# Separate buffers for the packed granules, the packed down weights and their repacked form, and a shift of when they are loaded, in a fused layernorm, S4 and int4 FFN kernel

## The chip, the cores and the metric

The kernel runs on one core of one Trainium2 chip. The metric is the device time of one execution in microseconds (us). A single profiled execution has its own time, which is given beside the median of the runs. Engines are called PE (TensorE), DVE (VectorE), ACT (ScalarE), POOL (GpSimd) and SP (SyncE, which here issues nearly all transfers, in one order, as a queue).

## The reference

One layer on an input of 2048 tokens by 1024 channels: a layernorm, and then the sum of the input, a state-space convolution (S4) and a gated feed-forward network (FFN) whose weights are 4-bit integers with a scale and a zero point for each group of 64.

```python
def dequantize(W_q, scale, zero):            # W_q: two 4-bit values per element
    hi = W_q >> 4 & 15
    lo = W_q & 15
    w = jnp.stack([hi, lo], axis=-1).reshape(out, half * 2).astype(scale.dtype)
    w = w.reshape(out, -1, GROUP)            # GROUP = 64
    return ((w - zero[:, :, None]) * scale[:, :, None]).reshape(out, half * 2)
...
g = jnp.einsum('bsh,ih->bsi', xn, dequantize(gate_Wq, ...))    # 2752 x 1024
u = jnp.einsum('bsh,ih->bsi', xn, dequantize(up_Wq, ...))
ffn = jnp.einsum('bsi,hi->bsh', silu(g) * u, dequantize(down_Wq, ...))
...
s4 = irfft(rfft(xn, 2 * L) * rfft(K, 2 * L))[..., :L] + D * xn  # K from the S4 parameters
return x + s4 + ffn
```

## The kernel before, in words

The weights come as 65 granules of 128x512 int32 (256 KB each; one int32 holds two 4-bit values). Granules 0 to 41 are the gate and up weights, two for each of the blocks 0 to 20; granule 42 is a mixed remainder; 43 to 62 are down weights in ten pairs; 63 and 64 are the last down weights (`G_WP` is 63). Gate/up and last granules also have a small tile of scales and zero points, sz.

A gate/up granule goes through these steps. `load_raw` (line 304) issues two transfers on SP, the packed granule into a tile raw and its sz. `unpack` (312) lets DVE split the 4-bit values into a tile w, two instructions. `scale_a` (346), called by `w_scale` in three parts of 4, 6 and 6 groups, lets ACT apply scale and zero point, 16 instructions. DVE then forms sums of quarters of w (`w_sums`), because the matrix product is done with seven products in place of eight. ACT writes the high half of each value in fp16 and DVE the rest (`w_hi`, `w_lo`, into tiles nat). `w_t` transposes the two nat tiles by DMA into a weight tile wf, which PE reads. There is a ring of four wf tiles; below, wf24 is the tile of granule 24.

The down granules are handled by `load_wd` (478), one unit u for each pair. `load` (485) brings the packed granule into a raw tile. `fetch_wd` (489) issues four transfers of scales into w, lets DVE split the packed values into int16 in a tile qn (two instructions), and transposes qn by DMA back into the raw tile. `dequant` (506) is two DVE instructions from that raw tile. Sums, `hi` (ACT) and `lo` (DVE, followed by a transfer to memory, WD) follow for seven parts. The two granules of the next unit are loaded and fetched in the course of the unit.

`gate_up` (623) is the main work on PE: for a block j and one half cp of the tokens it does seven products of 12 matmuls each (128x512), into the accumulation banks A, B, C and D; ACT copies banks between products (`A.copy(bD, bB)` gives "D<-B" in the trace) and DVE and ACT form the gated result in tiles ha, hb and s, which SP writes to memory (HF). One block takes about 36 us.

The loop at lines 1148 to 1169 runs over blocks 4 to 20 and both halves. Between the products of a half it advances the granules under way (`step_granules`), the down units (`wd_steps`) and the steps of the S4 kernel (`s4_steps`, tiles s4n, s4p). Here the instruction orders of DVE, ACT, PE and SP are pinned: every instruction of an engine is issued after the one that stands before it in the program (class `Engine`, 67 to 86). An instruction that waits therefore holds up all that stand behind it on that engine. All pinned instructions carry the line 82 in the profile, unpinned ones the line 77, and so tiles are told apart by name.

`granule` (1107) is the chain for one gate/up granule; each `yield` is one step. `queue` holds the granules still to do and `ahead` those that are loaded one ahead. Granule 63 is loaded in the loop just before its chain starts.

Buffers: `wtemp` (140) takes a tile from the pool in `home[kind]`. At line 1088 the kinds "raw" and "sz" get a pool raw2 on the left side of memory. Its ring of tag raw has four slots, which packed gate/up granules, packed down granules and qn tiles share in the order in which they are asked for; sz has two. A new tile in a slot waits for the last use of the old one.

```python
            szbufs[0] = 2
            home["raw"] = home["sz"] = more("left", "raw2", 4)
```

Of the kernel before, what the change touches and what calls it, by code (L numbers as in the profile page):

```python
# [26 lines left out]
I32 = mybir.dt.int32  # L27
I16 = mybir.dt.int16
# [5 lines left out]
P = 128  # L34
# [4 lines left out]
NJ = 21  # L39
# [3 lines left out]
G_WP = G_WD + 2 * NPAIR  # L43
# [5 lines left out]
SPG = 8  # L49
FETCH = {8: 15, 9: 15}  # L50
BEHIND = {4: 15}

XS = 64.0
WS = 1024.0
# [33 lines left out]
def build(nc, tc, x, xp, raw_d, sz_d, par_d, vct_d, tab_d, csrow_d, out):  # L88
# [3 lines left out]
    with es:  # L92
# [37 lines left out]
        right = lambda name, **k: ea.enter_context(tc.tile_pool(name=name, side="right", **k))  # L130
# [3 lines left out]

        we = ExitStack()
        weights = lambda side, name, **k: we.enter_context(tc.tile_pool(name=name, side=side, **k))
        home, szbufs = {"nat": weights("right", "nat", bufs=4)}, [4]
        home["raw"] = home["sz"] = home["w"] = weights("right", "dq", bufs=2)

        def wtemp(kind, shape, dtype, name):  # L140
            return home[kind].tile(shape, dtype, tag=kind, name=name, **({"bufs": szbufs[0]} if kind == "sz" else {}))

        early = ExitStack()
        hfp = early.enter_context(tc.tile_pool(name="hf", bufs=2))
# [155 lines left out]
        with ea:  # L300
# [1 line left out]
            rawt = {}  # L302

            def load_raw(gi):
                raw = wtemp("raw", [P, 16, 32], I32, f"raw{gi}")
                ld = SP
                ld.dma_start(raw, raw_d[gi].rearrange("p (a b) -> p a b", a=16))
                sz = wtemp("sz", [P, 2, 16], F32, f"sz{gi}")
                ld.dma_start(sz, sz_d[gi])
                return raw, sz  # L310
# [167 lines left out]
            def load_wd(u):  # L478


                pr, kq = divmod(u, 2)
                ga, gb = (G_WD + 2 * p + kq for p in (pr, pr + NPAIR // 2))
                tt, sub = V.tensor_tensor, ALU.subtract

                def load(gi):
                    raw = rawd[gi] = wtemp("raw", [P, 16, 32], I32, f"raw{gi}")
                    SP.dma_start(raw, raw_d[gi].rearrange("p (a b) -> p a b", a=16))

                def fetch_wd(gi):


                    raw = rawd.pop(gi)
                    w = wtemp("wd", [P, 8, 256], F32, f"w{gi}")
                    for i in range(2):
                        for b in range(2):
                            SP.dma_start(w[64 * b : 64 * b + 64, 4 * i : 4 * i + 4].rearrange("p f c -> p (f c)"),
                                        SZT[gi - G_WD, 1 - i, b].rearrange("c h -> (c h)").partition_broadcast(64))
                    q = wtemp("raw", [P, 16, 2, 32], I16, f"qn{gi}")
                    low = raw.bitcast(I16).rearrange("p a (b c) -> p a b c", c=2)[:, :, :, 0]
                    V.tensor_scalar(q[:, :, 0, :], low, 4, 15, ALU.logical_shift_right, ALU.bitwise_and)  # L500
                    V.tensor_scalar(q[:, :, 1, :], low, 15, None, ALU.bitwise_and)
                    qt = raw.bitcast(I16).rearrange("p a b -> p (a b)").rearrange("p (a b) -> p a b", a=8)
                    SP.dma_start_transpose(qt, q.rearrange("p a b c -> p (a b c)"))
                    return w, qt

                def dequant(w, qt):
                    x4 = w[:, 0:4]
                    tt(x4, qt.rearrange("p (f a) b -> p f (a b)", f=4), x4, sub)
                    tt(x4, x4, w[:, 4:8], ALU.mult)

                blocks = lambda w: w.rearrange("p f (m c) -> p f m c", m=2)
                nats = {}

                def hi(i, src):
                    nats[i] = wtemp("nat", [P, 7, 2, P], F16, f"nd{u}_{i}")
                    A.copy(nats[i][:, :, 0], src)

                def lo(i, src):
                    nat = nats.pop(i)
                    tt(nat[:, :, 1], src, nat[:, :, 0], sub)  # L520
                    SP.dma_start(
                        WD2[i - 1][:, :, pr, kq].rearrange("f p a c -> p f (a c)"), nat.rearrange("p f a c -> p f (a c)")
                    )

                nxt = [G_WD + 2 * ((u + 1) // 2 + o) + (u + 1) % 2 for o in (0, NPAIR // 2)] if u + 1 < NPAIR else None
                if u == 0:
                    load(ga)
                    load(gb)
                    yield
                    ready_wd[ga] = fetch_wd(ga)  # L530
                    yield
                    ready_wd[gb] = fetch_wd(gb)
                    yield
                ma = ready_wd.pop(ga)
                dequant(*ma)
                if nxt:
                    load(nxt[0])
                wa = blocks(ma[0][:, 0:7])
                yield
                sums(ma[0], True)  # L540
                hi(1, wa[:, :, 0])
                yield
                lo(1, wa[:, :, 0])
                tt(wa[:, :, 0], wa[:, :, 1], wa[:, :, 0], sub)
                hi(5, wa[:, :, 0])
                yield
                lo(5, wa[:, :, 0])
                yield
                mb = ready_wd.pop(gb)
                dequant(*mb)  # L550
                if nxt:
                    load(nxt[1])
                wb = blocks(mb[0][:, 0:7])
                yield
                sums(mb[0], True)
                hi(3, wb[:, :, 1])
                yield
                tt(wa[:, :, 1], wb[:, :, 1], wa[:, :, 1], sub)
                lo(3, wb[:, :, 1])
                hi(7, wa[:, :, 1])  # L560
                yield
                tt(wb[:, :, 1], wb[:, :, 1], wa[:, :, 0], sub)
                lo(7, wa[:, :, 1])
                hi(6, wb[:, :, 1])
                yield

                lo(6, wb[:, :, 1])
                hi(2, wb[:, :, 0])
                if nxt:
                    ready_wd[nxt[0]] = fetch_wd(nxt[0])  # L570
                yield
                lo(2, wb[:, :, 0])
                tt(wb[:, :, 0], wb[:, :, 0], wb[:, :, 1], sub)
                hi(4, wb[:, :, 0])
                yield
                lo(4, wb[:, :, 0])
                if nxt:
                    ready_wd[nxt[1]] = fetch_wd(nxt[1])
                yield
# [504 lines left out]
            we.close()  # L1084
            more = lambda side, name, bufs: weights(side, name, bufs=bufs, reuse_waits="tile")
            home["nat"], home["w"], home["wd"] = more("right", "nat2", 5), more("right", "w2", 1), more("right", "wd", 2)
            szbufs[0] = 2
            home["raw"] = home["sz"] = more("left", "raw2", 4)

            wd_steps = (None for u in range(NPAIR) for _ in load_wd(u))  # L1090
            s4_steps = s4()
# [15 lines left out]
            def granule(gi):  # L1107

                last_i = gi >= G_WP
                if not gi % 2:  # L1110
                    yield
                w_unpack(gi)
                w_scale(gi, 0)
                yield
                if gi + 1 in ahead:
                    rawt[gi + 1] = load_raw(gi + 1)
                w_scale(gi, 1)
                yield
                w_scale(gi, 2)
                yield  # L1120
                if not last_i:
                    w_sums(gi)
                yield
                wp_hi(gi - G_WP) if last_i else w_hi(gi)
                yield
                wp_lo(gi - G_WP) if last_i else w_lo(gi)
                if not last_i and gi % 2:
                    w_t(gi)
                yield
                yield  # L1130
                yield
                if not last_i and not gi % 2:
                    w_t(gi)
                yield
# [19 lines left out]
            for j in range(4, NJ):  # L1154
                for cp in range(2):
                    PE.pin = (j, cp) != (4, 0)
                    for n, _ in enumerate(gate_up(j, cp, wt[j])):
                        if n == 4 and queue:
                            if queue[0] == G_WP:
                                rawt[G_WP] = load_raw(G_WP)  # L1160
                            under_way.append(granule(queue.pop(0)))
                        if n == 2:
                            step_granules()
                        if n in (2, 4, 6) or n == 0 and waits is None:
                            next(wd_steps, 0)
                        if waits == "read" or n == 5 or n == 0 and cp and waits != "bank":
                            waits = s4_next()
                        if n != 2:
                            step_granules()
# [446 lines left out]
```

## Time and profile before

| what | value |
|---|---|
| median of 3 runs | 1281.69 us (1280.97 to 1282.39) |
| the profiled execution | 1286.51 us, its span 1284.7 us |
| mean granted clock of PE in it | 0.993 |
| PE busy | 1259.7 us, 98% of the span |
| DVE, ACT, POOL busy | 1020.2 us (79%), 676.5 us (53%), 184.3 us (14%) |
| HBM read and written | 132.88 MB and 94.84 MB |
| loads of packed granules (raw) | 65 of 256 KB, 4.0 us from issue to landing in the median |

A group of instructions in the profile is written engine, operation, out<-in, with the shapes as partitions x elements. An idle time stands in brackets behind an instruction, with the arrow to what ended it: "[0.47 <-ACT D L82]" says that the engine sat idle for 0.47 us until ACT's instruction on bank D. SPq is SP's queue, and its durations are those of issuing, not of the transfer.

### The profile page before, as it was taken

How to read it: one execution, taken by the hardware profiler on the slowest of the kernel's cores; microseconds unless marked ns; L12 is line 12 of the kernel's file. 1: busy time of each engine (PE TensorE's matmuls, PEld its weight loads, DVE VectorE, ACT ScalarE, POOL GpSimd, SP SyncE). 2: the span in 40 equal slices, each digit the busy share in tenths (PEclk: the TensorE clock that was granted, in tenths of full speed). 3: DMA queues.
4: the chain of work that ended last, by engine and by line, in shares of the span. 5: the costliest groups of instructions: out<-in, count | busy, mean ns of one | idle time of the engine just before them, and what ended most of it. 6: DMA issues, size and time to landing. Idle time of an engine off the chain costs nothing. (4 is left out here: it accounts for less than half of the span.)

```text
span 1284.7 us, 21385 instructions
## 1 busy us (share of the span) xinstructions
PE 1259.7 (98%) x8098; PEld 760.0 (59%) x8098; DVE 1020.2 (79%) x1391; ACT 676.5 (53%) x1219; POOL 184.3 (14%) x280
## 2 busy tenths in 40 slices
PE   7999899999999999999998999999999999999998
PEld 6644344444444444444443444467678888888887
DVE  7789975788888788779787886657669889779792
ACT  6777665665757656676576575620205433343330
POOL 2330010000010000101010001100000130366440
PEclk8999999999999999999998999999999999999999
DMA  6792829788895969799998998866868777999981
GB/s 233 195 209 50 184 92 207 191 227 207 207 252 133 266 148 247 192 224 248 238 243 198 260 246 185 251 231 200 307 201 317 254 236 217 257 288 257 289 175 50
DMA packets 358842, 276.59 MB, mean 215 GB/s; under 512 B 211851, under 2 KB 304851, under 8 KB 354643
## 3 DMA queue, kind: packets, MB, share of 16 engines
q1 hardware_dynamic: 336147, 263.17, 74.4%
q0 software_dynamic: 22016, 11.02, 7.1%
q8 instruction: 63, 1.03, 0.3%
q10 hardware_dynamic: 576, 1.05, 0.2%
q14 instruction: 40, 0.33, 0.1%
HBM read 132.88 MB, written 94.84 MB: 177 GB/s over the span
## 5 line engine op out<-in xcount | busy, mean ns | idle before, releaser
L82 PEld LDWEIGHTS <-wf 128*128 128x128 f16 x3000 | 287.3, 99 | 348.9 <-issue 11.5
L77 PEld LDWEIGHTS <-g 128*128 128x128 f16 x2940 | 287.6, 98 | 34.0 <-DVE g L77 0.6
L82 ACT ACTIVATE w<-w,sz 128x64 f32<-128x64 int32 x564 | 197.8, 428 | 66.8 <-DVE w L82 50.1
L82 PE MATMUL D<-x,wf 128*128 128x512 f16 x816 | 191.3, 385 | 2.2 <-ACT D L82 2.2
L77 PE MATMUL A<-b,g 128*128 128x256 f16 x1680 | 186.0, 273 | 0.3 <-DVE g L77 0.3
L82 PE MATMUL A<-x,wf 128*128 128x512 f16 x792 | 177.9, 380 | 5.0 <-DMA wf<-nat 4.6
L82 PE MATMUL C<-x,wf 128*128 128x512 f16 x804 | 179.1, 379 | 0.0
L77 ACT CAST g<-a 128x2560 f16<-128x2560 f32 x42 | 97.4, 2325 | 135.8 <-PE A L77 50.4
L82 DVE TENSOR_TENSOR w<-w 128x256 f32<-128x256 f32 (+1 forms) x244 | 132.7, 545 | 39.4 <-ACT w L82 32.3
L77 PEld LDWEIGHTS <-wf 128*128 128x128 f16 x960 | 86.0, 98 | 95.6 <-DMA wf<-nat 5.7
L77 DVE TENSOR_TENSOR g<-a,g 128x2560 f16<-128x2560 f32 x42 | 118.2, 2820 | 27.5 <-ACT g L77 27.5
L1468 POOL DMA_DIRECT2D out<-o x64 | 77.9, 2019 | 308.1 <-DVE o L77 288.3
L334 POOL TENSOR_SCALAR sz<-sz 128x16 f32<-128x16 f32 x43 | 19.4, 450 | 627.8 <-DMA sz<-in_sz 551.7
L82 ACT CAST nd<-w 128x896 f16<-128x896 f32 x70 | 65.3, 933 | 83.5 <-DVE w L82 70.0
L77 PE MATMUL D<-b,g 128*128 128x256 f16 x840 | 94.1, 273 | 0.0
L82 PE MATMUL B<-x,wf 128*128 128x512 f16 x396 | 90.9, 379 | 0.1
L82 DVE TENSOR_TENSOR nd<-w,nd 128x896 f16<-128x896 f32 x70 | 76.0, 1086 | 9.1 <-ACT nd L82 9.1
L82 ACT CAST nat<-w 128x896 f16<-128x896 f32 x62 | 55.3, 936 | 33.4 <-ACT B L82 17.0
L77 PEld LDWEIGHTS <-x 128*128 128x128 f16 x672 | 54.3, 98 | 20.9 <-issue 2.4
L82 DVE TENSOR_TENSOR nat<-w,nat 128x896 f16<-128x896 f32 x62 | 64.8, 1084 | 1.1 <-ACT nat L82 1.1
L77 DVE SCALAR_TENSOR_TENSOR p<-cv,p 128x512 f32<-128x512 f32 x32 | 22.0, 689 | 34.9 <-PE cv L77 23.4
L77 PE MATMUL cv<-band,x 128*128 128x256 f16 (+3 forms) x384 | 47.0, 272 | 2.0 <-DVE p L77 2.0
(181 smaller groups left out, 1451.1 us busy)
## 6 DMA issues: line engine op xcount, KB each, us to landing
a<-HF SPq DMA_DIRECT2D x28, 1280.0 KB, 7.4
WD<-nd SPq DMA_DIRECT2D x70, 448.0 KB, 4.0
b<-WD SPq DMA_DIRECT2D x49, 640.0 KB, 6.1
w<-SZT SPq DMA_DIRECT2D x80, 256.0 KB, 5.3
raw<-in_raw SPq DMA_DIRECT2D x65, 256.0 KB, 4.0
HF<-ha SPq DMA_DIRECT2D x54, 256.0 KB, 3.2
HF<-s SPq DMA_DIRECT2D x40, 256.0 KB, 3.2
HF<-hb SPq DMA_DIRECT2D x36, 256.0 KB, 3.2
```

Of the source, the lines that this page charges most:

```text
L77: return method(*args, **kw)
L82: self.last = method(*args, **kw)
L334: G.tensor_scalar(sz[:, 0], sz[:, 0], WS, None, ALU.mult)
L1468: G.dma_start(dst, o[:, q], accum_op=ALU.add)
```

## The change

A ring of four slots for all three kinds is replaced by kinds with buffers of their own: one for packed gate/up granules ("raw"), two for packed down granules ("rawd"), one for qn. The footprint is the same. Granules 8, 9 and 10 are loaded from this pool before the first down unit needs it; the dictionary `RAW` puts them into the buffers of the other two kinds.

With one buffer for a packed gate/up granule, the load of the next one moves in `granule` from before the second part of `w_scale` to before the third, one step later. Granules 63 and 64 are now among those that are loaded one ahead: granule 63 is loaded in the chain of granule 41, which is the one before it in the queue, and the separate load in the loop is gone. In `load_wd` the loads of the next unit's granules move from behind `dequant` to behind the first `lo` of the same granule, two steps later.

```diff
+RAW = {8: "qn", 9: "rawd", 10: "rawd"}
...
-        home, szbufs = {"nat": weights("right", "nat", bufs=4)}, [4]
+        home, own = {"nat": weights("right", "nat", bufs=4)}, {"sz": 4}
...
-            return home[kind].tile(shape, dtype, tag=kind, name=name, **({"bufs": szbufs[0]} if kind == "sz" else {}))
+            return home[kind].tile(shape, dtype, tag=kind, name=name, **({"bufs": own[kind]} if kind in own else {}))
...
             def load_raw(gi):
-                raw = wtemp("raw", [P, 16, 32], I32, f"raw{gi}")
+                raw = wtemp(RAW.get(gi, "raw"), [P, 16, 32], I32, f"raw{gi}")
...
                 def load(gi):
-                    raw = rawd[gi] = wtemp("raw", [P, 16, 32], I32, f"raw{gi}")
+                    raw = rawd[gi] = wtemp("rawd", [P, 16, 32], I32, f"raw{gi}")
...
-                    q = wtemp("raw", [P, 16, 2, 32], I16, f"qn{gi}")
+                    q = wtemp("qn", [P, 16, 2, 32], I16, f"qn{gi}")
...
                 dequant(*ma)
-                if nxt:
-                    load(nxt[0])
                 wa = blocks(ma[0][:, 0:7])
                 yield
                 sums(ma[0], True)
                 hi(1, wa[:, :, 0])
                 yield
                 lo(1, wa[:, :, 0])
+                if nxt:
+                    load(nxt[0])
...
                 dequant(*mb)
-                if nxt:
-                    load(nxt[1])
...
                 lo(3, wb[:, :, 1])
+                if nxt:
+                    load(nxt[1])
...
-            szbufs[0] = 2
-            home["raw"] = home["sz"] = more("left", "raw2", 4)
+            own.update(sz=2, raw=1, rawd=2, qn=1)
+            home["raw"] = home["sz"] = home["rawd"] = home["qn"] = more("left", "raw2", 1)
...
-                if gi + 1 in ahead:
-                    rawt[gi + 1] = load_raw(gi + 1)
                 w_scale(gi, 1)
                 yield
+                n = G_WP if gi == 2 * NJ - 1 else gi + 1
+                if n in ahead:
+                    rawt[n] = load_raw(n)
                 w_scale(gi, 2)
...
                         if n == 4 and queue:
-                            if queue[0] == G_WP:
-                                rawt[G_WP] = load_raw(G_WP)
                             under_way.append(granule(queue.pop(0)))
```

## The prediction

> **What bounds the kernel now.** I read the page first. TensorE (PE) is busy for 1259.7 of 1284.7 us, so at most 25 us can be had by removing waits anywhere, and every loss must appear as a new PE wait.
>
> ```profile
> span 1284.7 us, 21385 instructions
> PE 1259.7 (98%) x8098; PEld 760.0 (59%) x8098; DVE 1020.2 (79%) x1391; ACT 676.5 (53%) x1219; POOL 184.3 (14%) x280
> ```
>
> The change touches only the loop over blocks 4 to 20, which lies between 200 and 865 us. The table of windows gives PE 657.69 us busy there, so 665.00 - 657.69 = 7.3 us idle in that stretch. PE's list of waits for 160 to 870 us says on what:
>
> ```profile
> PE A L82 <- DMA wf<-nat: 4.6, 3, 2.9
> PE D L82 <- ACT D L82: 2.2, 1, 2.2
> PE cv L77 <- DVE p L77: 0.9, 1, 0.9
> PE A L82 <- DVE ha L82: 0.4, 1, 0.4
> ```
>
> The columns are total us, times, longest. The first line is weight tiles whose transposes land late (0.47 at block 12, 2.89 and 1.25 at block 17). The second is one wait at 800 us, the only one that the changed loads cause directly. The timeline from 788 to 802 us shows it:
>
> ```profile
> 792.60 1.68 SPq L82 DMA_DIRECT2D raw<-in_raw  x1
> ...
> 796.81 0.76 DVE L82 TENSOR_SCALAR w<-raw 128x512 int32<-128x512 int32 x2 [5.08 <-DMA raw<-in_raw]
> ...
> 798.30 1.43 ACT L82 ACTIVATE w<-w,sz 128x64 f32<-128x64 int32 x4 [9.99 <-POOL sz L336]
> ...
> 799.64 0.57 ACT L82 COPY D<-B 128x512 f32<-128x512 f32 x1
> 800.26 2.30 PE L82 MATMUL D<-x,wf 128*128 128x512 f16 x6 [2.22 <-ACT D L82]
> ```
>
> Granule 63 is loaded just before it is unpacked. VectorE (DVE) waits 5.08 us, ScalarE (ACT) stands behind it, ACT's copy into bank D comes late, and PE loses 2.22 us.
>
> The instruction orders of PE, DVE and ACT are the same in both builds; only SyncE's (SP's) queue is reordered and some waits differ. So the sum consists of (1) that load, (2) new waits for buffers, (3) weight transposes that meet other transfers ahead of them on SP.
>
> **The change part by part.**
>
> *1. Granule 63 loaded at granule 41, about one half-block earlier.* The 5.08 us on DVE and the 2.22 us on PE go. What is late next there: the block 20 weights, whose tile wf41 has 3.0 us between landing and need, and which now gets two loads ahead of it (0.42 + 0.40 us of issue by the 799 us pair): still 2 us in hand. I take **-2.2**, range -2.2 to -1.9.
>
> *2. One buffer for the repacked form (qn).* Of 40 instructions that write qn in 20 granules, four already waited for the previous granule's transpose; the tile's view says
>
> ```profile
>   DMA raw<-qn: 11.5, 4
> ...
> DMA to landing us min/median/max: 5.5/5.9/7.3
> ```
>
> In the four-slot ring the second qn of a pair mostly came to the slot of the first, so it waited already; I compared the waits of both builds, and only qn56 (block 11) is newly made to wait, for qn46's transpose. DVE's and then SP's timeline:
>
> ```profile
> 418.85 0.76 DVE L82 TENSOR_SCALAR qn<-raw 128x512 int16<-128x512 int16 x2
> ...
> 420.33 0.69 DVE L82 SCALAR_TENSOR_TENSOR hb<-hb,D 128x512 f32<-128x512 f32 x1 [0.47 <-ACT D L82]
> ...
> 435.81 0.76 DVE L82 TENSOR_SCALAR w<-raw 128x512 int32<-128x512 int32 x2 [2.90 <-DMA raw<-in_raw]
> ```
>
> ```profile
> 418.99 1.26 SPq L82 DMA_TRANSPOSE raw<-qn  x1
> ...
> 430.60 0.43 SPq L82 DMA_DIRECT2D raw<-in_raw  x1
> ...
> 431.86 1.27 SPq L82 DMA_DIRECT2D HF<-hb  x2
> ```
>
> qn46's transpose is issued at 418.99; two loads that now come ahead of it (raw22, sz22) add about 0.9; it lands 5.5 to 7.3 later, median 5.9, so at 425.8. DVE stood ready at 418.85: a stall of 6 to 7 us (bounds 419.9 + 5.5 - 418.85 = 6.6 and 8.4; without the 0.9, 5.6). DVE's order is fixed, so all behind it waits: the hb sum, the scaled weights, the second dequantisation. On its way the delay eats the idle time that DVE had: 0.47, 0.32 and 0.90 us up to 425, then 2.90 us at 435.81 for raw23. That last one is no free cover: raw23 itself is reissued behind the two HF transfers of 1.27 us and behind the late work, so it lands at 437.7 to 438.4, which agrees with 435.81 + 6.95 - 4.6 = 438.2. From there DVE and ACT run 2.0 to 2.6 us late. The next idle places on DVE (1.11 us at 442.31, 2.62 at 465.75) wait for ACT, which is delayed by the same chain, so they cover little. PE's margins down the road, each the need minus the end of its producer: 2.1 us at 441.4, 2.2 at 451.8, 1.7 for wf23 (458.2), 0.05 at 467.58, none at 477.08. PE's timeline there:
>
> ```profile
> 477.08 2.75 PE L82 MATMUL A<-x,wf 128*128 128x512 f16 x12 [0.38 <-DVE ha L82]
> ...
> 497.77 0.82 PE L82 MATMUL A<-x,wf 128*128 128x512 f16 x3 [0.47 <-DMA wf<-nat]
> ```
>
> So nearly the whole 2.0 to 2.6 reaches PE at 467 or 477: **+2.3**. Bounds: 3.5, if the landing takes 7.3 us and nothing is absorbed; and 0.5 from below, since a like wait, 4.08 us at 614.19, cost PE nothing, although there the next margins were wider (0.44 us at 627 and then none below 2). I stay near the upper part because 467.58 has no margin.
>
> A rule that speaks against this part: the Trainium skill, "Trainium Kernel Development and Optimization", Best Practices, advises two buffers so that transfers run beside computing. The row above, 11.5 us of DVE waiting in four places, agrees that a shared buffer makes DVE wait, but the 4.08 us of it at 614 cost PE nothing; by the rule every such wait is a loss and this part would cost all 6 to 7 us, by the row nothing.
>
> *3. wf25 (block 12).* SP's queue between the transposes of wf24 and wf25 (483.31 and 490.62) now holds raw26 and sz26, 0.9 us. PE already waits 0.47 there, so there is no margin. But if item 2 has delayed PE by 2.3, the need moves too, and only what the producers lose beyond that counts. I take **+0.7**; range -0.4 (the wait vanishes in PE's lateness) to +1.2.
>
> *4. wf35 (block 17).* raw51 leaves from ahead of these transposes:
>
> ```profile
> 676.19 0.39 SPq L82 DMA_DIRECT2D raw<-in_raw  x1
> ...
> 678.08 4.88 SPq L82 DMA_TRANSPOSE wf<-nat  x2
> ```
>
> Its 0.39 us and the gap of 0.09 behind it come off the 2.89 us wait: **-0.5**. Range -1.4 (also a 256 KB transfer less beside the transposes) to 0 (the weights themselves are late).
>
> *5. wf37 (block 18).* raw38 and sz38 (0.42 and 0.41 us at 700.70 and 701.22) now go between the two pairs of transposes at 702.80 and 714.78. The margin is 1.04 us and PE is 0.5 earlier by item 4: 0.83 + 0.5 - 1.04 = 0.3, with gaps between issues **+0.4**; range 0 to 0.9.
>
> *6. Other loads moved later.* Every gate/up granule is loaded one step later and every down granule about two. A load lands in 4.0 to 4.4 us; nearly all had 5 to 50 us in hand. The least is raw33, now behind a qn transpose: **0**, range 0 to +0.5. Odd weight tiles 13, 15, 19 and 39 lose a load ahead of them, but had margin: 0.
>
> Sum: -2.2 + 2.3 + 0.7 - 0.5 + 0.4 = **+0.7 us**. The profiled execution took 1286.51 us, 4.8 above the median of the runs, 1281.69; I put the change on both: 1287.2 profiled and **1282.4** as the median.
>
> **The rivals.** 0.2%, 2.56 us, is about what a measurement of this kernel can tell from no change; so 1279.1 to 1284.3 is "the same".
>
> *A, slower: the qn wait hits PE in full.* One place, block 11: if raw23's unpack starts more than 4.4 us late (after 440.2 instead of 438), PE's 0.05 us of margin at 467.58 passes everything on. With 4.4 in place of 2.3 the sum is +2.8, from which point it is slower; a landing of 7.3 us (+1.4) together with raw23 behind another HF issue of 1.27 makes item 2 5.0 and the sum +3.4: 1285.1. For it: no margin at two points. Against it: the median landing, 5.9.
>
> *B, faster: the qn wait is soaked up* as at 614.19. Then item 2 is 0 and PE keeps -2.2 - 0.5 + 0.4 + 0 to 0.7, so -2.3 to -1.6, or -2.7 if wf37 is in time: about 1279. If the 2.89 + 1.25 us at block 17 vanish too, because less is in flight, 1275.6. Against it: DVE's idle places behind 435 wait for ACT, which the same chain feeds.
>
> *C, the buffers do not matter.* PE is fed through a pipeline some 30 us deep; losses of 0.3 to 0.7 us on SP and the gain at 800 us cancel, or neither shows: 1281 to 1282. Same sign as my forecast, with no qn stall reaching PE.
>
> **How the numbers follow.** My forecast with its bounds (1279.5 to 1284.5) and C together 0.52; A 0.30; B 0.18, of which 0.05 below 1278. Range: with every item at its upper bound, and item 2 at 3.5, the sum is -1.9 + 3.5 + 1.2 + 0 + 0.9 + 0.5 = 4.2, 1285.9; B's 1279 without the 1.25 us at block 17 is 1277.7, and the rest of B lies below. So 1277.7 to 1286.0, which also holds A's 1285.1. Since A lies wholly above 1284.3 and B nearly wholly at or below 1279.1: faster 0.17, same 0.52, slower 0.31.
>
> **What the changed profile would show.** 1: no DVE wait for raw at 797, no PE wait for D at 800. 2: a DVE wait of 6 to 7 us for the transpose of qn near 419, the wait of 2.90 near 436 gone or smaller, new PE waits of 2 us at 467 or 477. 3: PE's wait for wf near block 12 about 1 us. 4: the 2.89 at block 17 near 2.4. 5: a PE wait below 1 us near 725. The qn tile's line should total about 18 us in 5 places. The forecast is wrong if the stall at 419 is absent, if it exceeds 8.4, or if transposes slow or speed up because other transfers now run beside them: SP's transposes take 4.3 to 6.3 us a pair, so each 1 us on wf25, wf35 or wf37 moves PE by about as much.

## The result, and the profile after

The changed kernel takes 1285.07 us (median of 17 runs, 1283.39 to 1286.72) against 1281.5 (17 runs of before, 1279.9 to 1284.73). The ratio is 1.0026, with a 95% interval of 1.0019 to 1.0032: slower by 3.3 us (3.6 between the medians). The profiled execution took 1286.03 us, 1.0 above its median.

The page of the changed kernel begins:

```profile
span 1284.3 us, 21381 instructions
PE 1258.2 (98%) x8098; PEld 759.2 (59%) x8098; DVE 1019.9 (79%) x1391; ACT 676.0 (53%) x1219; POOL 200.2 (16%) x280
```

The span is 0.4 us *shorter* than that of before, although the timed runs are 3.3 us longer. The profiled execution of before was an unlucky one, 5.0 us above its median, so the two spans cannot be set against each other. What can be compared is where each engine waits, and the time between the same two matmuls, since PE issues the same 8098 in both. PE's list of waits of the changed kernel, 160 to 870 us (total us, times, longest):

```profile
PE A L83 <- DMA wf<-nat: 5.0, 4, 3.4
PE B L83 <- ACT B L83: 1.7, 1, 1.7
PE D L83 <- ACT D L83: 1.5, 1, 1.5
PE C L83 <- DVE s4p L83: 0.9, 1, 0.9
PE A L83 <- DVE ha L83: 0.4, 1, 0.4
PE cv L78 <- DVE p L78: 0.2, 1, 0.2
```

The 2.2 us for bank D at 800 us is gone, as granule 63 is there in time; from the timeline of 788 to 806 us:

```profile
797.55 0.76 DVE L83 TENSOR_SCALAR w<-raw 128x512 int32<-128x512 int32 x2
...
802.82 2.75 PE L83 MATMUL D<-x,wf 128*128 128x512 f16 x12
```

In its place are waits at four places: 0.87 us for s4p at 427, 1.72 for bank B at 471, 1.54 for bank D at 633 (the "D" line above is this one), and for wf at 689, where the first of two waits grew from 2.89 to 3.39 us and the second fell from 1.25 to 0.63. (The other two in the line for wf are 0.31 us at 461 and 0.71 at 502, where before waited 0.47.) DVE's timeline of 414 to 445 us, and then SP's:

```profile
426.19 0.76 DVE L83 TENSOR_SCALAR qn<-raw 128x512 int16<-128x512 int16 x2 [7.41 <-DMA raw<-qn]
...
439.39 0.80 DVE L83 TENSOR_SCALAR w<-raw 128x512 int32<-128x512 int32 x2 [0.79 <-DMA raw<-in_raw]
```

```profile
420.86 1.26 SPq L83 DMA_TRANSPOSE raw<-qn  x1
...
431.25 1.99 SPq L83 DMA_DIRECT2D HF<-hb  x2
433.28 0.46 SPq L83 DMA_DIRECT2D raw<-in_raw  x1
```

The stall for the qn46 transpose is there, 7.41 us long, and raw23 is unpacked at 439.39 in place of 435.81, 3.6 us late, or 3.2 counted from the same matmul at 207 us, where this execution was 0.35 us behind. The second place is block 15; from the timeline of 618 to 634 us, SP, DVE, ACT and PE:

```profile
620.71 1.26 SPq L83 DMA_TRANSPOSE raw<-qn  x1
...
622.01 0.58 SPq L83 DMA_DIRECT2D raw<-in_raw  x1
...
629.26 0.76 DVE L83 TENSOR_SCALAR w<-raw 128x512 int32<-128x512 int32 x2 [1.29 <-DMA raw<-in_raw]
...
630.81 1.43 ACT L83 ACTIVATE w<-w,sz 128x64 f32<-128x64 int32 x4 [1.87 <-POOL sz L337]
...
632.78 1.45 PE L83 MATMUL D<-x,wf 128*128 128x512 f16 x6 [1.54 <-ACT D L83]
```

raw33 was issued ahead of the four scale transfers and the transpose of qn59 before; SP's timeline of before, 605 to 630 us:

```profile
611.23 2.43 SPq L82 DMA_DIRECT2D raw<-in_raw  x1
...
617.75 1.26 SPq L82 DMA_TRANSPOSE raw<-qn  x1
```

Now it stands behind them and lands some 7.2 us after its issue (622.01 to 629.26, where DVE had waited for it); ACT's scaling waits, its copy into bank D is late, and PE waits. The third place is block 17 in SP's queue:

```profile
673.58 6.14 SPq L83 DMA_TRANSPOSE wf<-nat  x2
679.78 0.98 SPq L83 DMA_DIRECT2D raw<-in_raw  x1
680.85 1.33 SPq L83 DMA_DIRECT2D sz<-in_sz  x1
...
684.37 4.63 SPq L83 DMA_TRANSPOSE wf<-nat  x2
```

The load that stands here between wf34 and wf35 is raw36, with sz36. raw51 has left from ahead of wf35, as forecast, but these two have come.

The table gives the time between the same matmuls of PE (the 1200th, 2180th, 2420th, 3200th, 3520th and 4000th; the times at the head are those of before) in the profiled execution of each kernel of the study. Ratios are to runs of before on the same chip. Ahead of the 1200th, where the kernels differ in little but the buffers that a few granules are loaded into, the executions differ by up to 5 us (204.8 to 210.0), which I leave out.

| kernel | 207 to 413 | 413 to 463 | 463 to 630 | 630 to 707 | 707 to 814 | timed ratio to before (95%) |
|---|---|---|---|---|---|---|
| before | 206.77 | 49.54 | 167.31 | 76.51 | 107.66 | 1 |
| changed | 206.77 | 51.13 | 170.85 | 75.95 | 103.60 | 1.0026 (1.0019 to 1.0032) |
| granule 63 ahead alone | 206.77 | 49.54 | 167.24 | 75.24 | 103.60 | 0.9983 (0.9973 to 0.9992) |
| buffers alone | 206.77 | 49.54 | 167.45 | 74.91 | 105.25 | 1.0002 (0.9992 to 1.0012) |
| buffers, 63 ahead | 206.77 | 49.54 | 167.88 | 74.97 | 103.60 | 0.9985 (0.9974 to 0.9995) |
| order and 63 ahead, one ring | 206.77 | 51.03 | 171.47 | 76.56 | 103.60 | 1.0019 (1.0006 to 1.0031) |
| five loads early | 206.77 | 49.54 | 168.27 | 74.49 | 103.60 | 0.9983 (0.9974 to 0.9991) |
| five loads later | 206.77 | 51.18 | 170.38 | 75.93 | 103.60 | 1.0033 (1.0022 to 1.0045) |
| gate/up loads later | 206.77 | 51.36 | 170.21 | 76.14 | 103.60 | 1.0033 (1.0020 to 1.0045) |
| down loads later | 206.77 | 51.36 | 168.26 | 74.58 | 103.60 | 0.9993 (0.9984 to 1.0002) |
| two loads early | 206.77 | 50.33 | 168.71 | 76.77 | 103.60 | 1.0011 (1.0002 to 1.0019) |
| four on POOL | 206.77 | 49.54 | 167.45 | 75.53 | 103.60 | 0.9986 (0.9974 to 0.9997) |
| two steps off | 206.77 | 49.55 | 168.03 | 69.07 | 105.92 | 0.9958 (0.9945 to 0.9972) |
| again at 20 | 206.77 | 49.61 | 168.39 | 69.07 | 104.47 | 0.9942 (0.9922 to 0.9962) |

The first column is the same to 0.01 us in all: differences in the others are effects of the change, of when transfers happened to land, or the clock. Against the kernel with the buffers and 63 ahead, the changed kernel loses 1.6, 3.0 and 1.0 us in the three stretches from 413 to 707. The profiled execution of before is 5.8 us longer than that of the kernel with the buffers alone: 1.6 us of it lie ahead of the 1200th matmul; 1.6 lie between 630 and 707, where the two wait alike (4.14 and 4.12 us) but the granted clock from 672 to 700 us was 0.88 against 0.94; and 2.4 lie in the last stretch, 0.7 of it a longer wait. PE's timeline of before at 800 us, and then of the kernel with the buffers alone at the same matmuls:

```profile
800.26 4.44 PE L82 MATMUL D<-x,wf 128*128 128x512 f16 x12 [2.22 <-ACT D L82]
```

```profile
796.50 2.75 PE L83 MATMUL D<-x,wf 128*128 128x512 f16 x12 [1.49 <-ACT D L83]
```

The same twelve matmuls take 1.69 us longer after the longer wait; the granted clock from 790 to 810 us was 0.91 in the first and 1.00 in the second.

### The profile page after: what moved, and what is told of

It is laid out like the page before. It is cut to its first block, busy times and chain, and to the rows that moved or that the text cites. A ratio compares the mean times of both kernels' runs of the same rounds, so it can differ in the third digit from the quotient of the medians.

```text
span 1284.3 us, 21381 instructions
## 1 busy us (share of the span) xinstructions
PE 1258.2 (98%) x8098; PEld 759.2 (59%) x8098; DVE 1019.9 (79%) x1391; ACT 676.0 (53%) x1219; POOL 200.2 (16%) x280
## 5 line engine op out<-in xcount | busy, mean ns | idle before, releaser
L83 PE MATMUL D<-x,wf 128*128 128x512 f16 x816 | 188.5, 381 | 1.5 <-ACT D L83 1.5
L335 POOL TENSOR_SCALAR sz<-sz 128x16 f32<-128x16 f32 x43 | 22.7, 527 | 617.1 <-DMA sz<-in_sz 547.2
```

Of the source, the lines that this page charges most:

```text
L83: self.last = method(*args, **kw)
L335: G.tensor_scalar(sz[:, 0], sz[:, 0], WS, None, ALU.mult)
```

## The experiments

### The change taken apart: ahead, buffers, order

Four kernels. The first is before with only the load of granule 63 moved. The second has the new buffers with every load where it was before; the third is the second with granule 63 ahead. The fourth has the new order and granule 63 ahead, in the old ring.

```diff
 # granule 63 ahead alone, to before
-                if gi + 1 in ahead:
-                    rawt[gi + 1] = load_raw(gi + 1)
+                n = G_WP if gi == 2 * NJ - 1 else gi + 1
+                if n in ahead:
+                    rawt[n] = load_raw(n)
...
-                            if queue[0] == G_WP:
-                                rawt[G_WP] = load_raw(G_WP)
 # buffers with 63 ahead, to the changed kernel (buffers alone: granule 63 late as well)
+                n = G_WP if gi == 2 * NJ - 1 else gi + 1
+                if n in ahead:
+                    rawt[n] = load_raw(n)
                 w_scale(gi, 1)
                 yield
-                n = G_WP if gi == 2 * NJ - 1 else gi + 1
-                if n in ahead:
-                    rawt[n] = load_raw(n)
...
                 dequant(*ma)          # and the same for mb, nxt[1] and lo(3)
+                if nxt:
+                    load(nxt[0])
...
                 lo(1, wa[:, :, 0])
-                if nxt:
-                    load(nxt[0])
 # order and 63 ahead, one ring, to the changed kernel
-            own.update(sz=2, raw=1, rawd=2, qn=1)
-            home["raw"] = home["sz"] = home["rawd"] = home["qn"] = more("left", "raw2", 1)
+            own.update(sz=2)
+            home["raw"] = home["sz"] = more("left", "raw2", 4)   # all kinds with the tag "raw"
```

> Before, with nothing changed but the load of granule 63, which now comes in the chain of granule 41. Theory 1 (the wait at 800 us of the profile of before is there in the timed executions too): the 2.2 us wait of PE for bank D goes, and the 1.7 us that PE then lost at 800 to 804 us at a lower granted clock (0.91 in 790 to 810 us, against 1.00 in the changed kernel) goes with it: 1277.6 to 1279.3 against 1281.5. Theory 2 (the profiled execution of before, 5 us above the median of its timed ones, had that wait by chance): 1281 to 1282, no change.

Measured: 1279.59 us, ratio 0.9983 (0.9973 to 0.9992), or -2.2 us. Between the two expectations and nearest to the wait itself: the load ahead gives its 2.2 us in timed runs, the further 1.7 us of clock, which that one execution lost, is not seen in them.

> The changed kernel with every load where it was before (and granule 63 late): the three kinds of buffers alone. Theory 1 (the new wait of qn56 for the transpose of qn46 costs most of the change's loss): DVE waits 6 to 7 us near 419 us, PE loses 1.7 to 2.8 us between 426 and 482, so 1283.2 to 1284.3 against 1281.5; the wait of 1.54 us at 631 us is not there, since granule 33 is loaded early again. Rival (the later loads cost it): 1281 to 1282. Open: each load of a down granule now waits in SP's queue for the dequantisation before it, up to 1 us for what stands behind it.

Measured: 1281.9 us, ratio 1.0002 (0.9992 to 1.0012). My theory falls. DVE's list of waits has the new wait of qn56, 5.8 us, as its longest, and qn waits 16.8 us in five places, but PE's list has only 0.2 us behind it. The lines of this kernel for DVE, and then for PE:

```profile
DVE qn L83 <- DMA raw<-qn: 16.8, 5, 5.8
```

```profile
PE A L83 <- DMA wf<-nat: 4.6, 3, 3.0
PE D L83 <- ACT D L83: 1.5, 1, 1.5
...
PE B L83 <- ACT B L83: 0.2, 1, 0.2
```

The page "Trainium Kernel Development and Optimization" of the Trainium skill (Best Practices) advises two buffers. Here the one buffer made DVE wait 5.8 us more, and the timed cost was 0.0002 +- 0.001 of 1282 us: the measurement decides, and at a stall of this length the second buffer was not needed.

> The changed kernel with its buffers and with granule 63 loaded ahead, all other loads where they were before. Theory 1 (qn wait costs 1.7 to 2.8, the load ahead gives 2.2 to 3.9): 1279.5 to 1282. If the load ahead gives nothing in timed executions: 1283.2 to 1284.3. If the later loads are what costs: as the kernel with the load ahead alone.

Measured: 1280.16 us, ratio 0.9985 (0.9974 to 0.9995), the same as with the load ahead alone. DVE's timeline of this kernel, 414 to 445 us, shows why the stall is free:

```profile
424.59 0.76 DVE L83 TENSOR_SCALAR qn<-raw 128x512 int16<-128x512 int16 x2 [6.19 <-DMA raw<-qn]
...
436.91 0.77 DVE L83 TENSOR_SCALAR w<-raw 128x512 int32<-128x512 int32 x2
```

6.19 us of stall leave w23 only 1.1 us later than before (435.81): the rest went into idle times that DVE had anyway, the 2.90 us for raw23 above all. raw23 is loaded at 429.83 here, and DVE no longer waits for it. PE loses 0.6 us at 468, 0.5 more than before.

> The changed kernel with its order of loads, but one ring of four buffers for all three kinds. By the waits of the build, qn53, qn56, qn59 and qn60 wait for no transpose here. Theory 1 (qn wait is the cost): no DVE wait near 419, no PE loss of 1.7 to 2.8 us between 426 and 482; the wait of 1.54 us at 631 us may stay: 1281.5 to 1283.4. Rival (the later loads are the cost): 1284.5 to 1286, as the changed kernel.

Measured: 1284.4 us, ratio 1.0019 (1.0006 to 1.0031). The rival holds: with no wait of qn56 at all, the order of loads alone turns 0.9983 into 1.0019, 4.6 us. In this kernel's timeline DVE runs freely at 417 and then waits for raw23 instead:

```profile
417.69 0.75 DVE L83 TENSOR_SCALAR qn<-raw 128x512 int16<-128x512 int16 x2
...
438.30 0.76 DVE L83 TENSOR_SCALAR w<-raw 128x512 int32<-128x512 int32 x2 [6.15 <-DMA raw<-in_raw]
```

The late load holds w23 until 438.30 (this execution was 0.7 us ahead at 207 us), whether DVE has stalled before it or not.

### Which loads

Starting from the buffers with 63 ahead (1280.2), one kernel moves only the gate/up loads one step later, and one only the down loads two steps. Then the changed kernel with two, and with five of its gate/up loads put back; and the reverse, only those five later.

```diff
 # two early (five early: the list is 22, 23, 26, 33, 36), to the changed kernel
+                n = G_WP if gi == 2 * NJ - 1 else gi + 1
+                if n in (23, 33):
+                    rawt[n] = load_raw(n)
                 w_scale(gi, 1)
                 yield
-                n = G_WP if gi == 2 * NJ - 1 else gi + 1
-                if n in ahead:
+                if n in ahead and n not in (23, 33):
                     rawt[n] = load_raw(n)
 # five later, to the buffers with 63 ahead
-                if n in ahead:
+                if n in ahead and n not in (22, 23, 26, 33, 36):
                     rawt[n] = load_raw(n)
                 w_scale(gi, 1)
                 yield
+                if n in (22, 23, 26, 33, 36):
+                    rawt[n] = load_raw(n)
```

> The new buffers and granule 63 ahead, loads of the down granules early as before, loads of the gate/up granules one step later. Theory (the later gate/up loads are the loss: raw23 behind two HF transfers, raw33 behind the qn59 transpose, raw36 and sz36 ahead of wf35): nearly all of the 4.9 us between 1280.2 and 1285.1 comes, 1284 to 1285.5; in the trace PE waits about 1 us at 426, 1.7 at 470, 1.5 at 631, 3.4 at 686. Rival (the down loads share it): 1281 to 1283.

Measured: 1285.14 us, ratio 1.0033 (1.0020 to 1.0045). The whole loss is here; PE waits 1.1 us at 426, 1.5 at 469, 1.0 at 631 and 4.3 at 688.

> The new buffers and granule 63 ahead, gate/up loads where they were before, loads of the down granules two steps later. Theory (the gate/up loads are the loss): no loss, 1279.5 to 1280.8; wf35 loses raw51 from ahead of its transposes, so PE's wait at block 17 is 0.5 us shorter than 2.8. Rival (the down loads share the loss): 1282 to 1284.

Measured: 1280.77 us, ratio 0.9993 (0.9984 to 1.0002), 0.0008 above the kernel that it starts from, with intervals that overlap. In timed runs the down loads have no share that can be told from nothing. Its profiled execution did lose 1.8 us between 413 and 463, behind a longer stall; DVE's timeline and then PE's, 404 to 470 us:

```profile
425.60 0.76 DVE L83 TENSOR_SCALAR qn<-raw 128x512 int16<-128x512 int16 x2 [7.83 <-DMA raw<-qn]
```

```profile
426.67 5.34 PE L83 MATMUL C<-x,wf 128*128 128x512 f16 x24 [1.66 <-DVE s4p L83]
```

It is not shown that the down loads did this: the kernel with five loads early, below, has them later as well, and there the stall was 5.94 us and PE did not wait for s4p.

> The changed kernel with only the loads of granules 23 and 33 where they were before; the other gate/up loads and all down loads stay later. Theory (two loads carry the loss): PE's waits of 0.6 us more near 460, 1.1 at 470 and 1.5 at 631 go; those at 426 (0.9, the qn46 transpose is still issued behind raw22) and 0.6 more at block 17 (raw36 ahead of wf35) stay: 1285.1 - 3.2, so 1281.5 to 1282.5. Rival (the loss is spread over many loads): 1284 to 1285.

Measured: 1283.09 us, ratio 1.0011 (1.0002 to 1.0019). The wait at 631 is gone and that at 470 is 1.1 us; 0.0015 of the 0.0041 between the changed kernel and the one with early loads came back, less than I expected. PE still waits 3.3 us at 687, with raw36 and sz36 ahead of wf35.

> The changed kernel with the loads of granules 22, 23, 26, 33 and 36 where they were before; all other gate/up loads and all down loads stay later. Theory (these five loads, each of which comes ahead of something with no margin or is itself late, carry the loss): as the kernel with the new buffers and all loads early, 1280 to 1281. Rival (the loss is spread): 1282 to 1283.5, between that kernel's 1280.2 and the 1283.1 with two loads early.

Measured: 1279.55 us, ratio 0.9983 (0.9974 to 0.9991). Everything came back.

> The reverse: the new buffers, granule 63 ahead and all loads early, but the loads of granules 22, 23, 26, 33 and 36 one step later. Theory: these five alone bring the loss, 1284 to 1285.5. Rival: 1281 to 1283.

Measured: 1285.43 us, ratio 1.0033 (1.0022 to 1.0045). Five loads of 32, one step later, are the loss, and without them there is none. Two runs say so from both sides. How the part beside granules 23 and 33 divides among 22, 26 and 36 was not tried.

The traces say one thing more of the stall of qn56. In the six profiled executions in which it was 5.8 to 6.3 us (buffers alone, buffers with 63 ahead, five early, four on POOL, two steps off, again at 20), PE did not wait for s4p behind it; in the five in which it was 7.4 to 7.8 us (changed, gate/up later, down later, two early, five later), PE waited 0.6 to 1.7 us. In four of these five, raw22 is loaded late, ahead of the transpose of wf that stands before that of qn46. So a stall of some 6 us is nearly all soaked up (0.2 to 0.8 us of waiting for bank B at 468 is left), and of one of 7.4 us and more a larger part reaches PE.

### What the largest wait is made of

PE's largest wait, at block 17, is in both kernels. Two tries on it, from the buffers with 63 ahead: one lets POOL issue the HF writes of the second half of block 15, and one leaves out two steps of the down units in block 16, so that later steps of theirs come later. A last kernel adds two such steps in block 19.

```diff
 # four on POOL
-                SP.dma_start(HF[cp][f, :, j // 2, :], src)
+                (G if (j, cp) == (15, 1) else SP).dma_start(HF[cp][f, :, j // 2, :], src)
 # two steps off (again at 20: (19, 0, 6) and (19, 1, 0) as well)
-                        if n in (2, 4, 6) or n == 0 and waits is None:
+                        if (n in (2, 4, 6) or n == 0 and waits is None) and (j, cp, n) not in ((16, 0, 6), (16, 1, 0),):
                             next(wd_steps, 0)
```

> The new buffers and granule 63 ahead, all other loads early as before (1280.2), and the four HF writes that stand ahead of wf35's transposes issued by POOL in place of SP. They take 3.2 us of SP's queue; so wf35's first transpose is issued about 3 us earlier and PE's waits of 2.8 and 1.1 us at 681 to 686 us nearly go, and with them some of the lower granted clock that follows (0.88 in 672 to 700 us): 1275 to 1277. Rival (the transposes are slow because the DMA engines are full, not because of the queue): 1279.5 to 1280.5.

Measured: 1279.74 us, ratio 0.9986 (0.9974 to 0.9997), as without it. SP's timeline of the kernel without, and then of this one:

```profile
669.02 6.08 SPq L83 DMA_TRANSPOSE wf<-nat  x2
...
678.66 5.27 SPq L83 DMA_TRANSPOSE wf<-nat  x2
```

```profile
667.96 8.44 SPq L83 DMA_TRANSPOSE wf<-nat  x2
...
677.13 6.14 SPq L83 DMA_TRANSPOSE wf<-nat  x2
```

The four HF writes no longer stand between the pairs, but the pairs take 2.4 and 0.9 us longer, and wf35 goes out 1.5 us earlier, 0.8 counted from the same matmul at 207 us. PE's wait for wf fell from 4.4 us to 3.3 in all, and no timed gain is seen. The page "DMA: Bandwidth & Descriptors" of the Trainium skill (Issuing engines are not separate DMA queues) says that transfers started by different engines share the same 16 DMA engines and interleave, and that only the time to issue is saved. This run fits that, with pairs 2.4 and 0.9 us longer and no timed gain; it does not show the sharing itself.

> The new buffers, granule 63 ahead, all loads early (1280.2), and two steps of the down units left out in block 16 and made up behind it, so that the four scale transfers of w60 (2.9 us of SP's queue) and the transpose of qn60 (1.3 us) come behind the transposes of wf35 and not ahead of those of wf34. Theory (what stands between 655 and 683 us on SP and on the DMA engines makes wf34 and wf35 late): PE's waits of 2.8 and 1.1 us at block 17 go, and some 1 to 2 us of lower clock behind them: 1274.5 to 1277. Rival (the shift makes other transposes late in blocks 17 to 20, since every later step of the down units moves by two): 1279 to 1284.

Measured: 1276.27 us, ratio 0.9958 (0.9945 to 0.9972), better than both kernels. SP's timeline:

```profile
663.61 4.69 SPq L83 DMA_TRANSPOSE wf<-nat  x2
...
671.91 5.18 SPq L83 DMA_TRANSPOSE wf<-nat  x2
...
677.79 2.82 SPq L83 DMA_DIRECT2D w<-SZT  x4
680.71 1.51 SPq L83 DMA_TRANSPOSE raw<-qn  x1
```

wf35 goes out 6.8 us earlier than in the kernel without the gap, 6.0 counted from the same matmul at 207 us. The windows of 672 to 700 us, of the changed kernel and of this one (PE busy and count first, the granted clock third from the end):

```profile
672.00:700.00 28.00, 23.99 (x100) 9.96 (x98) 23.63 (x37) 16.76 (x35) 2.18 (x6) 0.88 0.99 235
```

```profile
672.00:700.00 28.00, 28.00 (x132) 12.65 (x131) 23.16 (x36) 16.58 (x40) 1.56 (x3) 1.00 0.87 213
```

PE does not wait at all in that window, and runs at the full clock (24.11 us busy at 0.94 in the kernel without the gap). The stretch of 630 to 707 is 5.9 us shorter than without the gap, and that of 707 to 814 is 2.3 us longer, with new waits for wf at 790. With w60's scale transfers and qn60's transpose, a WD write and raw51 also left from ahead of wf35; the gain was not divided among them.

> The kernel with two steps of the down units left out in block 16 (1276.3), and two more left out in block 19 in the same places. In that kernel w62's four scale transfers and qn62's transpose stood ahead of the transposes of wf40 and wf41, as those of w60 had stood ahead of wf34 and wf35, and PE waited 0.28 and 1.38 us for wf at 790 us. Theory (the same cause): both waits go, 1.7 us and something of a lower clock less, 1273.5 to 1275. Rival (the last down unit now ends too late for the stage that follows, which reads WD): 1276 to 1280.

Measured: 1277.07 us, ratio 0.9942 (0.9922 to 0.9962) to the runs of before on its chip (1283.66), against 0.9958 for the kernel without the second gap: the intervals overlap. The waits of 1.7 us at 790 are gone, but PE now waits 0.6 us for wf at 754, 0.3 for the transfer of band at 833 and 1.3 for DVE at 855. A small gain is neither shown nor excluded.

## Why the prediction was right or wrong

The time, 1285.07, lies in the range (1277.7 to 1286.0), but the likeliest case, no change, did not come: it is slower by 0.26%, just beyond the bound of 0.2%. The sum was +0.7 us and should have been +3.3. Rival A named 1285.1, which is the measured time only by luck: its cause was the qn wait reaching PE in full, with raw23 unpacked after 440.2; it was unpacked at 439.39, and the wait by itself, in the kernel with the buffers alone, cost nothing that could be told.

*Item 1, -2.2:* right. The load alone gave -2.2 us in timed runs.

*Item 2, +2.3:* the stall was right in size (7.41 us, forecast near 7.0, at most 8.4) and PE lost about what I said behind it (0.87 + 0.31 + 1.72 us of waits), but not for the reason given. With the buffers alone the cost is 0.0002 +- 0.001, about 0.3 us, and 0.2 us of PE wait in the trace: rival B, that the wait is soaked up, was right for the buffers. The step that failed is "raw23 itself is reissued behind the two HF transfers of 1.27 us and behind the late work": I counted the move of that load as part of the stall. It is a cost of its own, and it needs no stall: in the kernel with the new order and the old ring, raw23 holds DVE until 438.30. I also judged PE's margins only by the work of the FFN; the copy s4p<-s4s, which stands right behind the stall on DVE and for which PE's next product C waited 0.87 us, was not in the sum. That wait is the stall's own, and came only where it was over 7 us long.

*Item 3, +0.7:* PE waits 0.71 for wf25 in place of 0.47: +0.24, inside the range.

*Item 4, -0.5:* what I counted came, and what I left out was larger. With only the down loads later, raw51 has left, and the stretch of 630 to 707 took 74.58 us against 74.97 (one execution each). But raw36 and sz36 come to stand ahead of wf35, 0.98 and 1.33 us in SP's queue, and of these I had nothing. In the five kernels that have them there the stretch took 75.9 to 76.8 us; in the six others with PE waiting there, before left out, 74.5 to 75.5. So this part was some +1 us and not -0.5. The waits alone do not show it, with 4.02 us in the changed kernel, 4.14 in the profile of before and 3.88 with early loads: most of the difference is the lower clock behind them, 0.88 against 0.94 (672 to 700 us), and before itself had 0.88 in its one profile.

*Item 5, +0.4:* no PE wait near 725: 0.

*Item 6, 0 to +0.5:* the bound was too small. raw33 cost 1.54 us of PE time, and the 1.29 us wait of DVE and the 1.87 of ACT behind it show how. I named the load as the one with the least in hand, and did not work out where it would be issued: the scale transfers of w59 and the transpose of qn59, issued from 617.60 to 621.97, stand ahead of it. I also took 4.0 to 4.4 us for its landing, which are medians (the view of raw before has 2.5 to 8.4), and it took some 7.2.

So my sum of the order's parts was about +0.6 (items 3 to 6), where the runs show 5 to 6 us: 0.9985 to 1.0026 for the whole order, 0.9985 to 1.0033 when the gate/up loads alone move. And the profiled span would have misled: by it the change is 0.4 us faster.

## What to carry to other kernels

When a load moves one step later in a shared queue, list every transfer that it falls behind and every one that it now stands ahead of, and price each at its own place: here 27 of 32 such moves cost nothing that could be measured, and five cost 5 to 6 us. A stall of 6 us on an engine whose next instructions wait for something else anyway can be free, and one of 7.5 us in the same place not; a load that arrives 3 us late just ahead of work with no margin is not. Where a transfer is late behind others, look at what can be moved behind it before asking which engine issues it: here the first gave 3.5 us and the second nothing, in one try each.

## What the runs showed of the hardware that was not expected

A PE wait costs more than itself in some executions. After 2.22 us of waiting twelve matmuls took 4.44 us at a granted clock of 0.91 (790 to 810 us), after 1.49 us of waiting they took 2.75 at 1.00. The length of the wait does not decide it: behind the two waits of block 17 the granted clock from 672 to 700 us was 0.88 in before (4.14 us of waiting), 0.94 in the kernel with the buffers alone (4.12 us) and 0.88 with the four writes on POOL (3.0 us). The page "TensorE: Matmul & The Clock Gate" of the Trainium skill (Part 1) ties the clock to how busy PE was in a window of about 3.4 us that runs freely. That equal waits cost more in one execution than in another would fit it, but no run here shows the window itself.

Two transposes of a pair took SP from 3.6 us (757 us in the changed kernel) to 8.4 us to issue. The longest was the pair at 668 us that met four more writes, those moved to POOL.
